# Where two norm averages and a row of products are written, and when four sums are made, in a kernel of two attention blocks

## The chip, the cores and the metric

The kernel runs on one core of a Trainium2 chip. A core has a TensorE (PE, the matmuls; PEld is its weight load), VectorE (DVE), ScalarE (ACT), GpSimdE (POOL) and SyncE (SP, which issues the DMAs). Matmuls write into PSUM, eight banks of 512 float32 for each of 128 partitions; VectorE and ScalarE read it from there. The metric is the device time of one execution in microseconds. One execution was profiled; in the text, times within it are counted from the start of its span.

## The reference, cut to what matters

The input x has 8 samples of 512 channels by 32 x 32 positions (1024 positions). Two layers follow each other:

```
# layer 0: 32 groups of 16 channels, 8 heads of 64 channels
h = group_norm(x, norm_w, norm_b)                  # mean and var over 16 channels x 1024
q, k, v = heads of (qkv_w @ h + qkv_b)
attn = softmax(q @ k.T / sqrt(64))                 # per head, 1024 x 1024
x = x + proj_w @ (attn @ v) + proj_b

# layer 1: one group of all 512 channels, one head
n = (x - mean(x)) * rsqrt(var(x) + eps) * gn_gamma + gn_beta
q, k, v = wq @ n + bq, wk @ n + bk, wv @ n + bv
attn = softmax(q.T @ k * 512**-0.5)                # 1024 x 1024
x = x + wo @ (v @ attn.T) + bo
```

All of it is float32.

## The kernel before, in words

The samples run one after the other, B = 8, each through `layer0` (from L651) and `attention1` (from L873). In layer 1 the weights are joined ahead of the loop: K's weight is multiplied into Q's (`wqk1`), and the output projection into V's (`wvo1`), by `product` (L581). Layer 1's norm is not applied to x: Q is made of raw x, and the norm comes in as a constant for each channel (`norm.c`) and a factor in the softmax. So the mean and the variance are needed only when the first finished parts of Q are scaled.

Large products are made by Strassen's scheme (`strassen`, L411), with seven multiplications of half size in place of eight. Each of the two operands is taken in quarters; of the weight the sums S1 to S4 are made (`finish`, L187), of the data T1 to T4 (`Combined.make`, L391: T1 = B12 - B11, T2 = B22 - T1, T3 = B22 - B12, T4 = B21 - T2). VectorE makes them all. One run of `strassen` is a generator of a group of output channels (or positions). It takes two PSUM tiles of two banks each, one with the tag "s" and one with the tag "o", and uses the first bank of each: `line` and `single`. Each tag has two tiles. The second bank of the "o" tile is left over and is remembered in `spare`. The order of one group is: A11·B11 into `line`, which ScalarE copies out (u1); A12·B21 into `single`, and VectorE adds u1 to it (`done(0, 0)`); S1·T1 into `single`; S2·T2 onto `line`, copied (u2); S3·T3 onto `line`, copied (u3), and `done(1, 1)`; A22·T4 onto `line`, `done(1, 0)`, then S4·B22 onto `single`, `done(0, 1)`.

`together` (L450) runs two such groups in turn, one piece of each: step 0 is the first piece of group 0, step 1 the first of group 1, step 2 the second of group 0 (S1·T1), step 3 that of group 1, steps 4 and 5 are S2·T2, 6 and 7 are S3·T3, 8 and 9 the rest. `at_steps` (L461) calls other work, the hooks, after the step whose number they have. As VectorE, ScalarE and TensorE take their instructions in the order in which the program issues them (`manual_schedule`, L1048), the step of a hook is its place in three queues at once. The DMA queue of SP is ordered by a planner.

Small matmuls that need a bank for a moment ask `room` (L279). It gives the spare bank if there is one. Both groups of `together` set `spare`, so from step 1 on it is the second group's. The users are:

- `group_average` (L283) and `sample_average` (L293), which average statistics over partitions with one matmul. `Norm.mean_of_all` (L322) and `Norm.deviation` (L332) call them, for the mean and the variance; in `deviation` POOL takes the power -0.5 afterwards.
- `through_q` (L1084), once, which multiplies the norm's and the bias's vectors into the joined Q weight (`Rows`, L551, 24 small matmuls), copies the rows out, stores them, and scales the weight's rows on ScalarE (L232).
- the row of biases `bias0` (L727) and the sums of `sum_both` (L815) for the next sample.

In `attention1` the Q stage (L903) makes Q in two groups, with T1 after step 0, the mean and T2 after step 1, the variance after step 3, and after step 4 `untaken` (four small constants), the two scaled products that were put off (`later`), and T3; T4 follows after step 6. V, the scores, the exponentials and the values come after it.

At the start of the program the Q and K weights of layer 0 are used for the first sample at L1101. Ahead of it stand `norm.normed` (x times scale plus shift), `wvo1.finish` (S1 to S4 of the joined V weight, and its store to DRAM), and `taken`, which copies the joined Q weight out of the four banks that the first Q and K use next. The weights live in a pool of three buffers (`wpool`), so `load_first("v0")` gets its buffer when an earlier weight is done with.

Of the kernel before, what the change touches and what calls it, by code (L numbers as in the profile page):

```python
# [65 lines left out]
def two_attention_blocks(  # L66
# [31 lines left out]
    def banks(tag, name):  # L98
        return psum.tile([P, 2, HALF], FP, tag=tag, name=name)
# [39 lines left out]
    nv1, wo1, nq1, nk1 = (raw(name) for name in ["nv1", "wo1", "nq1", "nk1"])  # L139
# [111 lines left out]
    waiting = []  # L251
# [24 lines left out]
        else:  # L276
            nc.scalar.copy(dst, src)

    def room(name):  # L279

        return banks("s", f"ps_{name}")[:, 0, :] if spare[0] is None else spare[0]

    def group_average(stat, name):  # L283

        ps = room(name)
        nc.tensor.matmul(
            ps[:, :NC], in_group.rearrange("p g s -> p (g s)"), stat, start=True, stop=True
        )
        mean = small.tile([P, NC], FP, tag="mean", name=f"mean_{name}")
        nc.vector.tensor_copy(mean, ps[:, :NC])  # L290
        return mean

    def sample_average(stat, name):  # L293

        ps = room(name)
        nc.tensor.matmul(ps[:, :NC], in_sample, stat, start=True, stop=True)
        mean = small.tile([P, 1], FP, tag="mean1", name=f"mean_{name}")
        nc.vector.tensor_reduce(mean, ps[:, :NC], AX.X, ALU.add)
        return mean
# [76 lines left out]
    def norm1(xs, b):  # L376
        return Norm(xs, sample_average, f"1_{b}")
# [28 lines left out]
            self.make(4)  # L406


    spare = [None]

    def strassen(multiply, done, name):  # L411

        us = {}

        def copied(n):
            us[n] = tile_u(f"u{n}_{name}")  # L420
            nc.scalar.copy(us[n], line)  # L421

        line = banks("s", f"ps_{name}_0")[:, 0, :]
        single = banks("o", f"ps_{name}_1")
        single, spare[0] = single[:, 0, :], single[:, 1, :]
        multiply(line, "A11", "B11", True)
        copied(1)
        multiply(single, "A12", "B21", True)
        done(0, 0, single, us[1])
        yield  # L430
        multiply(single, "S1", "T1", True)
        yield
        multiply(line, "S2", "T2", False)
        copied(2)
        yield
        multiply(line, "S3", "T3", False)
        copied(3)
        done(1, 1, single, us[3])
        yield
        multiply(line, "A22", "T4", False)  # L440
        done(1, 0, line, None)
        multiply(single, "S4", "B22", False)
        done(0, 1, single, us[2])
        yield
# [5 lines left out]
    def together(*groups):  # L450

        groups = list(groups)
        while groups:
            for g in list(groups):
                if next(g, g) is g:
                    groups.remove(g)
                else:
                    yield
        spare[0] = None

    def at_steps(steps, hooks):  # L461

# [188 lines left out]
    def layer0(bs, qs, ks, b, norm_next):  # L651
# [67 lines left out]
        ps = {}  # L719
# [17 lines left out]
        if norm_next is not None:  # L737
            hooks[4] = [lambda: norm_next.mean_of_all()]
            hooks[5] = [lambda: norm_next.variance_of_all()]
            combine = Combined(f"0_{b + 1}")  # L740
# [9 lines left out]
        norm = norm1(xs, b)  # L750
# [31 lines left out]
        for i in range(2, len(units) + 2):  # L782
# [4 lines left out]
            name = f"0_{b}_{pair}_{g}"  # L787
            if kt == NT - 1 and pair == end:
                if last:
                    ps_sum = banks("o", f"ps_sum_{name}")[:, 0, :]  # L790
# [13 lines left out]
        if b == 0:  # L804
            rows, = throughs
# [3 lines left out]
        if not last:  # L809

            name = f"0_{b}_{end}"
# [13 lines left out]
        later = []  # L825

        def project(w, c):
            def done(i, half, bank, u):
                chunk = c + 2 * i
                x = piece(xs, chunk, half)  # L830

                def add():
                    nc.vector.scalar_tensor_tensor(
                        x, bank if u is None else u, bias[:, chunk : chunk + 1], x, ALU.add, ALU.add
                    )
                    norm.of_half(chunk, half)


                first = last and i == half == 0
                if first and c == 0:  # L840
                    ps_sum = spare[0]
                    add_keys(end, [1], ps_sum)
                    combine1()
                    combine2(2, 0)
                    combine2(3, 0)
                if u is not None:
                    nc.vector.tensor_tensor(u, bank, u, ALU.add)
                if not first:
                    add()
                    return  # L850
                later.append(add)
                if c == 0:
                    invs[end] = one_over(ps_sum, f"0_{b}_{end}_1")
                    divide(end, 1, invs[end])
                else:

                    held(flat(accs[end, 1]), f"acc_0_{b}_{end}", flat(accs[end, 1]))
                    for n, k in [(2, 1), (3, 1), (4, 0), (4, 1)]:
                        combine2(n, k)
                    for more in later:  # L860
                        more()

            return strassen(by_channels(w, c, comb), done, f"p_0_{b}_{c}")
# [9 lines left out]
    def attention1(xs, norm, b, at_values):  # L873
# [5 lines left out]
        combine, later = Combined(f"1_{b}"), []  # L879
# [3 lines left out]
        def make_q(c):  # L883
# [18 lines left out]

        at_steps(together(make_q(0), make_q(1)), {  # L903
            0: [lambda: combine.make(1)],
            1: [norm.mean_of_all, lambda: combine.make(2)],
            3: [norm.deviation],
            4: [norm.untaken, lambda: later.pop(0)(), lambda: later.pop(0)(), lambda: combine.make(3)],
            6: [lambda: combine.make(4)],
        })
        bias = norm.bias()  # L910
        vs = blank(NT // 2, f"v_1_{b}")
# [12 lines left out]
        ps = [[[tile2(f"p_1_{b}_{j}{k}{i}") for i in range(2)] for k in range(2)] for j in range(2)]  # L924
# [65 lines left out]
        invs, later = [], []  # L990

        def values(c):
            def multiply(bank, a, b, fresh):
                for kt in range(NT // 2):
                    nc.tensor.matmul(  # L995
                        bank, v_parts[kt // 2][a][:, kt % 2, c * P : (c + 1) * P],
                        p_parts[kt // 2][b][:, kt % 2, :], start=fresh and kt == 0,
                        stop=kt == NT // 2 - 1, skip_group_check=True,
                    )

            def done(i, j, bank, u):
                first = i == j == 0
                if first and c == 0:
                    ps = spare[0]
                    for half in range(2):
                        nc.tensor.matmul(  # L1006
                            ps[half * HD : (half + 1) * HD, :], ones[:, :HD], acc[:, half, :],
                            start=True, stop=True,
                        )
                chunk = c + 2 * i  # L1010
                x = piece(xs, chunk, j)
                if u is None:
                    u = tile_u(f"o_1_{b}_{chunk}_{j}")
                else:
                    nc.vector.tensor_tensor(u, bank, u, ALU.add)
                    bank = u
                if first and c == 0:
                    held(ps, f"sum_1_{b}")
                    invs.append(one_over(ps, f"1_{b}"))
                    invs.append(spread(invs[0], HD, lambda i: [(i, r) for r in range(2)], f"1_{b}"))  # L1020

                def add():
                    nc.vector.scalar_tensor_tensor(
                        u, bank, norm.rstd, invs[1][:, j, :], ALU.mult, ALU.mult
                    )
                    nc.vector.scalar_tensor_tensor(
                        x, u, bias[:, chunk : chunk + 1], x, ALU.add, ALU.add
                    )

                if first:  # L1030
                    later.append(add)
                else:
                    add()

            return strassen(multiply, done, f"o_1_{b}_{c}")
# [9 lines left out]
    made, throughs = {}, []  # L1045


    with tc.manual_schedule(engines={PE, ACT, DVE}):  # L1048
        norm = norm0(xs_next, 0)
# [5 lines left out]
        wvo1 = Weight("wvo1")  # L1055
        product(wvo1, nv1, wo1, "o")()
        waiting.append(load_first("qk02"))
        wqk1 = Weight("wqk1")
        spare[0] = banks("o", "ps_norm")[:, 0, :]
        norm1_vectors = many(V_NB1, "norm1", V_NW1)  # L1060
        bias_v, bias_q = many(V_BV1, "bias_v", 0), many(V_BQ1, "bias_q", 0)

# [19 lines left out]
            throughs.append(Through(wvo1, bias_v, wo1, "v", banks("o", "ps_rows")[:, 0, :]))  # L1082

        def through_q():  # L1084
            throughs.append(Through(wqk1, bias_q, nk1, "q", room("rows")))

        taken = product(wqk1, nq1, nk1, "s", {
            (0, 1): [through_v], (1, 3): [norm.mean_of_all], (2, 1): [norm.variance_of_all]
        })
        spare[0] = None  # L1090
        norm.normed(xs_next)
        wvo1.finish()
        taken()
        waiting.append(load_first("v0"))
        ahead = [norm0(load_x(1, nc.sync), 1)]
        combine = Combined("0_0")
# [2 lines left out]
        qs, ks = [None] * NC, [None] * NC  # L1099
        w = next_weight()  # L1100
        at_steps(together(*pairs_qk(w, 0, combine.parts, qs, ks, 0)), {  # L1101
            1: [lambda: combine.make(3), through_q], 2: [lambda: combine.make(4)], 4: [wqk1.finish],
            8: [waiting[0].finish],
        })
        bs = combine.parts
        for rows in throughs:
# [1 line left out]
        for b in range(B):  # L1108
            if 0 < b < B - 1:
                ahead = [norm0(load_x(b + 1, nc.sync), b + 1)]  # L1110
            xs, norm, qs, ks = layer0(bs, qs, ks, b, ahead[0] if b + 1 < B else None)
# [24 lines left out]
        ps = banks("o", "ps_good")[:, 0, :]  # L1136
# [414 lines left out]
```

## Time and profile before

| what | value |
|---|---|
| median of 3 runs | 2943.11 us (2942.21 to 2943.16) |
| the profiled run, and its span | 2942.51 us, 2940.8 us |
| PE busy | 2906.7 us, 99% of the span |
| DVE busy | 1725.9 us, 59% |
| ACT busy | 1091.1 us, 37% |
| POOL busy | 14.2 us |
| from one V stage of layer 0 to the next sample's | 431.85 to 792.08 us, so 360.2 us |
| the Q stage of layer 1 in sample 1 | 643.65 to 670.40 us |

A line of the timeline has the start, the length, the engine, the line of the kernel, the operation, the tile that is written and those that are read, partitions and elements, and how many such instructions were merged. In square brackets stands how long the engine was idle before, and who ended that. In the chain of work that ended last, each piece has its start and its length. In a list of waits, the columns are the total in us, how often, and the longest. A float32 matmul shows as two records.

### The profile page before, as it was taken

Reading aid. Unit: us, or ns where it says so; the run is one execution under the profiler, and the core shown is the slowest. Engines: PE = TensorE matmul, PEld = TensorE weight load, DVE = VectorE, ACT = ScalarE, POOL = GpSimd, SP = SyncE. Lnnn points to the kernel's source line nnn. Section 1 sums busy time; section 2 is a strip of 40 time slices with the busy share of each in tenths; the row PEclk is TensorE's granted clock in tenths of the full one; section 3 lists DMA queues with packets and bytes.
Section 4 is the critical chain, followed back from the end, with each engine's and each line's share of the span. In section 5 each row is a group of like instructions: output and inputs, shape, how many; then the busy total and the mean of one; then the engine's idle time right before and its main releaser. Section 6 shows DMA issues by size and latency. Waiting matters only on the chain.

```text
span 2940.8 us, 34098 instructions
## 1 busy us (share of the span) xinstructions
PE 2906.7 (99%) x14050; PEld 1356.5 (46%) x14050; DVE 1725.9 (59%) x2147; ACT 1091.1 (37%) x1512; POOL 14.2 (0%) x28
## 2 busy tenths in 40 slices
PE   8999999999999999999999999999999999999998
PEld 4534544345543455334553355533545335453353
DVE  4676365853667536675367753577545764537835
ACT  2362324623246231552315523165222642226431
POOL 0000000000000000000000000000000000000000
PEclk9999999999999999999999999999999999999999
DMA  6401122011220112202031020310212111111001
GB/s 232 180 18 62 50 80 93 23 58 50 93 80 22 58 51 93 87 16 80 27 118 62 15 82 27 117 62 22 75 54 89 64 42 67 48 68 55 8 1 37
DMA packets 70724, 188.74 MB, mean 64 GB/s; under 512 B 18464, under 2 KB 18976, under 8 KB 64160
## 3 DMA queue, kind: packets, MB, share of 16 engines
q1 hardware_dynamic: 70416, 186.46, 18.9%
q8 instruction: 112, 1.84, 0.3%
q14 instruction: 52, 0.43, 0.1%
q10 hardware_dynamic: 144, 0.02, 0.0%
HBM read 137.43 MB, written 28.57 MB: 56 GB/s over the span
## 4 chain that ended last, share of the span: by engine, by line
PE 97%; DVE 2%; ACT 0%; issue 0%; SPq 0%; DMA 0%; POOL 0%; DVEq 0%; ACTq 0%; POOLq 0%
PE s L677 15%; PE ps_o L696 15%; PE ps_v L489 13%; PE ps_o L995 13%; PE ps_s L938 13%; PE ps_q L474 13%; PE ps_k L474 7%; PE ps_p L474 6%; PE ps_sum L710 1%; PE ps_wvo L589 1%; DVE u_q L887 0%; DVE inv L619 0%; DVE t L397 0%; PE ps_o L1006 0%; DVE acc L608 0%; PE ps_wqk L589 0%
## 5 line engine op out<-in xcount | busy, mean ns | idle before, releaser
L606 ACT ACTIVATE p<-s 128x1024 f32<-128x1024 f32 x512 | 523.8, 1025 | 316.2 <-PE s L677 313.5
L677 PE MATMUL s<-q,k 64*64 64x512 f32 x4096 | 532.2, 591 | 0.0
L696 PE MATMUL ps_o<-p,v 64*64 64x512 f32 x4096 | 528.7, 589 | 0.0
L608 DVE TENSOR_TENSOR acc<-acc,p 128x1024 f32<-128x1024 f32 x384 | 468.6, 1220 | 86.2 <-ACT p L606 69.9
L677 PEld LDWEIGHTS s<-q,k 64*64 64x64 f32 x4096 | 152.6, 133 | 292.9 <-issue 258.3
L696 PEld LDWEIGHTS ps_o<-p,v 64*64 64x64 f32 x4096 | 156.6, 133 | 282.8 <-issue 280.3
L946 DVE TENSOR_TENSOR p<-ps_s,u_s 128x512 f32<-128x512 f32 x96 | 66.4, 692 | 246.8 <-ACT u_s L421 140.9
L523 DVE TENSOR_TENSOR v<-ps_v,u_v 128x512 f32<-128x512 f32 x96 | 66.2, 690 | 197.6 <-PE ps_v L489 126.3
L421 ACT COPY u_v<-ps_v 128x512 f32<-128x512 f32 x96 | 56.3, 586 | 305.8 <-PE ps_v L489 305.8
L938 PE MATMUL ps_s<-s_q,t 128*128 128x512 f32 x384 | 167.4, 592 | 0.0
L995 PE MATMUL ps_o<-t_p,s_v 128*128 128x512 f32 x384 | 166.1, 592 | 0.0
L421 ACT COPY u_q<-ps_q 128x512 f32<-128x512 f32 x96 | 56.0, 583 | 272.8 <-PE ps_q L474 272.8
L608 DVE TENSOR_TENSOR acc<-p,p 128x1024 f32<-128x1024 f32 x64 | 78.4, 1225 | 98.9 <-ACT p L606 98.9
L474 PE MATMUL ps_q<-t,w_wqk 128*128 128x512 f32 x256 | 116.8, 600 | 7.3 <-DVE t L397 7.3
L948 ACT ACTIVATE p<-p,factor 128x512 f32<-128x512 f32 x96 | 69.3, 722 | 133.2 <-DVE p L946 133.2
L938 PEld LDWEIGHTS ps_s<-s_q,t 128*128 128x128 f32 x384 | 73.0, 190 | 91.8 <-issue 91.8
L995 PEld LDWEIGHTS ps_o<-t_p,s_v 128*128 128x128 f32 x384 | 73.0, 190 | 91.8 <-issue 87.3
L995 PE MATMUL ps_o<-p,v 128*128 128x512 f32 x256 | 113.3, 595 | 0.0
L474 PE MATMUL ps_p<-t_p,w_p 128*128 128x512 f32 x256 | 112.6, 593 | 0.7 <-DVE inv L619 0.7
L489 PE MATMUL ps_v<-w_wvo,t 128*128 128x256 f32 x512 | 113.1, 379 | 0.0
L938 PE MATMUL ps_s<-q,x 128*128 128x512 f32 x256 | 112.5, 592 | 0.0
L315 DVE BATCH_NORM_STATS2 part<-x 128x6 f32<-128x512 f32 x128 | 85.4, 687 | 35.0 <-DMA x<-in_x 32.7
(226 smaller groups left out, 3564.6 us busy)
## 6 DMA issues: line engine op xcount, KB each, us to landing
x<-in_x SPq DMA_DIRECT2D x92, 512.0 KB, 7.3
w_qk<-stored_qk SPq DMA_DIRECT2D x14, 1792.0 KB, 7.4
out<-x SPq DMA_DIRECT2D x32, 512.0 KB, 2.8
inv<-inv SPq DMA_DIRECT2D x248, 64.0 KB, 2.0
w_wqk<-stored_wqk SPq DMA_DIRECT2D x8, 1792.0 KB, 7.6
w_wvo<-stored_wvo SPq DMA_DIRECT2D x8, 1792.0 KB, 7.2
w_v<-stored_v SPq DMA_DIRECT2D x7, 1792.0 KB, 7.1
w_p<-stored_p SPq DMA_DIRECT2D x7, 1792.0 KB, 7.2
```

The costliest lines, as they stand in the source:

```text
L315: nc.vector.bn_stats(self.part[:, cc, half, :], piece(self.xs, cc, half))
L421: nc.scalar.copy(us[n], line)
L474: nc.tensor.matmul(bank, w[a][:, k, c * P : (c + 1) * P], bs[b][:, k, :], start=fresh and k == 0, stop=k == 1, skip_group_check=True,)
L489: nc.tensor.matmul(bank[:, u * 2 * P : (u + 1) * 2 * P], bs[b][:, k, n * P : (n + 1) * P], w[a][:, k, :], start=fresh and u == k == 0, sto ...
L606: nc.scalar.activation(p, s, AF.Exp, scale=factor)
L608: nc.vector.tensor_tensor(acc, first, p, ALU.add)
L677: nc.tensor.matmul(s[cols, j, :], flat(ks[pair])[rows, k0 : k0 + HD], qs[pair][rows, g, :], start=True, stop=True,)
L696: nc.tensor.matmul(o[cols, half, :], vs[kt][rows, c0 : c0 + HD], p[rows, j, :], start=kt == 0, stop=kt == NT - 1,)
L938: nc.tensor.matmul(bank, bs[b][:, k, t * P : (t + 1) * P], q_parts[a][:, k, :], start=fresh and k == 0, stop=k == 1, skip_group_check=True,)
L946: nc.vector.tensor_tensor(p, bank, u, ALU.add)
L948: nc.scalar.activation(p, bank, AF.Exp, scale=norm.factor)
L995: nc.tensor.matmul(bank, v_parts[kt // 2][a][:, kt % 2, c * P : (c + 1) * P], p_parts[kt // 2][b][:, kt % 2, :], start=fresh and kt == 0, ...
```

## The change

`spare`, one place, becomes `spares`, a list with the left-over bank of each group that runs. `room` takes a number: the norm averages and `through_q` ask for the first group's bank, the other callers still get the latest one. In the Q stage of layer 1 the mean goes from step 1 to step 2, T3 from step 4 to 2, the variance from step 3 to 4, T4 from step 6 to 4, and the constants with the two scaled products from step 4 to 5. At the start, `wvo1.finish` goes from ahead of `taken` to step 3 of the first Q and K, `through_q` from step 1 to step 2, there ahead of T4, and `wqk1.finish` from step 4 to step 5.

```diff
@@ -276,13 +276,13 @@
         else:
             nc.scalar.copy(dst, src)
 
-    def room(name):
-
-        return banks("s", f"ps_{name}")[:, 0, :] if spare[0] is None else spare[0]
+    def room(name, n=-1):
+
+        return spares[n] if spares else banks("s", f"ps_{name}")[:, 0, :]
 
     def group_average(stat, name):
 
-        ps = room(name)
+        ps = room(name, 0)
         nc.tensor.matmul(
             ps[:, :NC], in_group.rearrange("p g s -> p (g s)"), stat, start=True, stop=True
         )
@@ -292,7 +292,7 @@
 
     def sample_average(stat, name):
 
-        ps = room(name)
+        ps = room(name, 0)
         nc.tensor.matmul(ps[:, :NC], in_sample, stat, start=True, stop=True)
         mean = small.tile([P, 1], FP, tag="mean1", name=f"mean_{name}")
         nc.vector.tensor_reduce(mean, ps[:, :NC], AX.X, ALU.add)
@@ -406,7 +406,7 @@
             self.make(4)
 
 
-    spare = [None]
+    spares = []
 
     def strassen(multiply, done, name):
 
@@ -422,7 +422,8 @@
 
         line = banks("s", f"ps_{name}_0")[:, 0, :]
         single = banks("o", f"ps_{name}_1")
-        single, spare[0] = single[:, 0, :], single[:, 1, :]
+        spares.append(single[:, 1, :])
+        single = single[:, 0, :]
         multiply(line, "A11", "B11", True)
         copied(1)
         multiply(single, "A12", "B21", True)
@@ -450,13 +451,14 @@
     def together(*groups):
 
         groups = list(groups)
+        spares.clear()
         while groups:
             for g in list(groups):
                 if next(g, g) is g:
                     groups.remove(g)
                 else:
                     yield
-        spare[0] = None
+        spares.clear()
 
     def at_steps(steps, hooks):
 
@@ -838,7 +840,7 @@
 
                 first = last and i == half == 0
                 if first and c == 0:
-                    ps_sum = spare[0]
+                    ps_sum = spares[0]
                     add_keys(end, [1], ps_sum)
                     combine1()
                     combine2(2, 0)
@@ -902,10 +904,10 @@
 
         at_steps(together(make_q(0), make_q(1)), {
             0: [lambda: combine.make(1)],
-            1: [norm.mean_of_all, lambda: combine.make(2)],
-            3: [norm.deviation],
-            4: [norm.untaken, lambda: later.pop(0)(), lambda: later.pop(0)(), lambda: combine.make(3)],
-            6: [lambda: combine.make(4)],
+            1: [lambda: combine.make(2)],
+            2: [norm.mean_of_all, lambda: combine.make(3)],
+            4: [norm.deviation, lambda: combine.make(4)],
+            5: [norm.untaken, lambda: later.pop(0)(), lambda: later.pop(0)()],
         })
         bias = norm.bias()
         vs = blank(NT // 2, f"v_1_{b}")
@@ -1001,7 +1003,7 @@
             def done(i, j, bank, u):
                 first = i == j == 0
                 if first and c == 0:
-                    ps = spare[0]
+                    ps = spares[0]
                     for half in range(2):
                         nc.tensor.matmul(
                             ps[half * HD : (half + 1) * HD, :], ones[:, :HD], acc[:, half, :],
@@ -1056,7 +1058,7 @@
         product(wvo1, nv1, wo1, "o")()
         waiting.append(load_first("qk02"))
         wqk1 = Weight("wqk1")
-        spare[0] = banks("o", "ps_norm")[:, 0, :]
+        spares.append(banks("o", "ps_norm")[:, 0, :])
         norm1_vectors = many(V_NB1, "norm1", V_NW1)
         bias_v, bias_q = many(V_BV1, "bias_v", 0), many(V_BQ1, "bias_q", 0)
 
@@ -1082,14 +1084,12 @@
             throughs.append(Through(wvo1, bias_v, wo1, "v", banks("o", "ps_rows")[:, 0, :]))
 
         def through_q():
-            throughs.append(Through(wqk1, bias_q, nk1, "q", room("rows")))
+            throughs.append(Through(wqk1, bias_q, nk1, "q", room("rows", 0)))
 
         taken = product(wqk1, nq1, nk1, "s", {
             (0, 1): [through_v], (1, 3): [norm.mean_of_all], (2, 1): [norm.variance_of_all]
         })
-        spare[0] = None
         norm.normed(xs_next)
-        wvo1.finish()
         taken()
         waiting.append(load_first("v0"))
         ahead = [norm0(load_x(1, nc.sync), 1)]
@@ -1099,8 +1099,8 @@
         qs, ks = [None] * NC, [None] * NC
         w = next_weight()
         at_steps(together(*pairs_qk(w, 0, combine.parts, qs, ks, 0)), {
-            1: [lambda: combine.make(3), through_q], 2: [lambda: combine.make(4)], 4: [wqk1.finish],
-            8: [waiting[0].finish],
+            1: [lambda: combine.make(3)], 2: [through_q, lambda: combine.make(4)],
+            3: [wvo1.finish], 5: [wqk1.finish], 8: [waiting[0].finish],
         })
         bs = combine.parts
         for rows in throughs:
```

## The prediction

> **What bounds the kernel now.** I read the page first: busy shares, then the chain that ended last.
>
> ```profile
> span 2940.8 us, 34098 instructions
> PE 2906.7 (99%) x14050; PEld 1356.5 (46%) x14050; DVE 1725.9 (59%) x2147; ACT 1091.1 (37%) x1512; POOL 14.2 (0%) x28
> PE 97%; DVE 2%; ACT 0%; issue 0%; SPq 0%; DMA 0%; POOL 0%; DVEq 0%; ACTq 0%; POOLq 0%
> ```
>
> TensorE sets the end. The change removes no large matmul, so only two things can pay: time in which TensorE stands still, and time at a lower clock. Next I asked for all waits, and kept those of PE:
>
> ```profile
> PE ps_q L474 <- DVE t L397: 7.3, 8, 0.9
> PE ps_q L296 <- DVE u_q L887: 6.8, 8, 0.9
> ```
>
> Both occur eight times, once a sample, in the Q stage of the second layer, which the change edits. The PE timeline of sample 1's stage:
>
> ```profile
> 643.65 7.03 PE L474 MATMUL ps_q<-x,w_wqk 128*128 128x512 f32 x16
> 651.54 0.39 PE L296 MATMUL ps_q<-stat,in_sample 128*128 128x4 f32 x2 [0.85 <-DVE u_q L887]
> 651.78 3.68 PE L474 MATMUL ps_q<-t,w_wqk 128*128 128x512 f32 x8
> 655.30 0.28 PE L296 MATMUL ps_q<-spread,in_sample 128*128 128x4 f32 x2
> 655.44 7.11 PE L474 MATMUL ps_q<-t,w_wqk 128*128 128x512 f32 x16
> 663.46 1.95 PE L474 MATMUL ps_q<-t,w_wqk 128*128 128x512 f32 x4 [0.91 <-DVE t L397]
> ```
>
> The last rows of this stage end where V begins, at 670.40. A 512-column record takes 0.429 us from start to start (663.46 to 665.25 holds four, with a slow first). The stage takes 670.40 - 643.65 = 26.75 us for 56 such records, which is 24.03; 2.72 us are something else. The chain in the same stretch says what:
>
> ```profile
> 650.79 0.70 DVE u_q L887
> ...
> 660.87 0.60 ACT u_q L421
> 661.47 0.02 issue
> 661.49 0.69 DVE u_q L887
> 662.18 1.14 DVE t L397
> ```
>
> The mean's matmul waits for the second group's sum u_q to be read out of the bank beside it; T4 stands in VectorE's queue behind a u_q that needs ScalarE's copy.
>
> The third place is the start, once. The chain from 20 to 70 us:
>
> ```profile
> 35.75 0.61 DVE w_wvo L188
> ...
> 38.28 0.61 DVE rest_wqk L599
> 38.89 0.04 issue
> 38.94 5.40 PE ps_q L474 x8
> ...
> 47.87 0.76 DVE k L506
> 48.64 0.14 issue
> 48.77 1.96 PE ps_k L551 x24
> ```
>
> Four sums of wvo (35.75 to 38.28) stand ahead of the copy that frees the first Q's bank, and the vectors' products wait for k's sum. Its first eight matmuls take 5.40 us instead of 3.43; a stage table over that stretch gives the granted clock, 0.67, after PE's busy time:
>
> ```profile
> 39.00:44.10 5.10, 5.10 (x8) 2.13 (x9) 5.00 (x10) 0.59 (x1) 0.00 (x0) 0.67 1.02 360
> ```
>
> **The Trainium skill.** "PSUM — Partial Sum Buffer", section "PSUM bank collisions raise a hardware error", says to guard PSUM by bank (and quadrant), not address. The trace is stricter: the mean's matmul waits 0.85 us for a read of the other bank of its two-bank tile, so the wait follows the tile. "TensorE: Matmul & The Clock Gate", section "What's actually happening", says an idle window of about 3.4 us halves the array's clock for the next, and that windows run freely. The trace agrees roughly: 2.04 us of idleness before 38.94 was followed by the half clock, while 2.44 us before 115.75 was not (granted clock 1.00 from 92.1 to 121.4). The same page (section "Architectural detail: the array is 16× 32×32, not 1× 128×128") calls VectorE and ScalarE strict FIFO; T4's place agrees. "DMA: Bandwidth & Descriptors", section "Issuing engines are not separate DMA queues", says that all transfers share 16 engines: a stored_qk at 47.48 and rows_q at 51.40 agree, rows_q taking 10.0 us to land against 2.0 for rows_v.
>
> **The change, Q stage, eight times.** Take PE's end of the first 16 records, 643.65 + 16 x 0.429 = 650.52. New order: group 0's S1·T1 to 652.24 (T1 ready at 649.25), then the mean's pair. It writes group 0's tile, last read at 648.12, and its statistics are ready: no wait. A pair costs 0.14 plus a slow start of about 0.09 (group norm's pairs at 104.12 and 106.06 do just that), so 0.23. Group 1's S1·T1 to 654.2; group 0's S2·T2 to 655.9 (T2 now directly follows u_q, ready near 652.7); the variance's pair (spread ready near 653.5); group 1's S2·T2 to 657.8. T3 runs on DVE near 653.5 to 654.7, needed at 657.8. T4 follows the variance's small operations, near 656.6 to 657.8, instead of 663.3; needed at 661.3.
>
> What is queued behind: on DVE the four constants (about 0.7 us) now wait for T4, so they end near 658.4 instead of 657.37; POOL's power (0.55 us) moves a step and overlaps T4. On ACT the two scaled products (1.52) now follow group 1's copy, to 660.0, and group 0's third copy (0.59) ends near 660.6. Its line is written again at 661.3: 0.7 us of slack, so I cost it at nothing, hidden by group 1's S3·T3. The held u buffers: five exist; the sixth request comes after the first scaled product. Result 24.03 + 2 x 0.23 = 24.48; gain 26.75 - 24.48 = 2.27 a sample, bounds 1.1 (ACT takes T4's place) to 2.72 (the pairs cost nothing). Times eight: 18.2 us. V, scores and the rest follow PE, so all shifts.
>
> **Group norm of the next sample** merely moves to q's spare bank. Its pairs waited for nothing before and q's sum is read long before: nothing, hidden in PE's stream.
>
> **The start.** ACT's copies of the K product begin at 36.67; DVE's copy of the same bank follows ACT's (as wvo's at 21.13 did), so it ends near 37.95 rather than 38.88: Q starts at 38.0, gain 0.9. PE then idles 1.1 us instead of 2.04, and I expect the full clock: gain 4 x 0.43 = 1.7. q and k end near 44.9. The vectors' products go after q's S1·T1 into q's tile, read near 44.5: the k wait (1.00 plus a slow start, 1.17) goes. Sum 3.8. Row copy and eight scalings on ACT (0.59 and 8 x 0.40) end near 52.7, and q's second copy follows at 53.3, 0.3 before PE needs its line: nothing. wqk's sums (4 x 0.6) run to 55.2, before q's third copy: nothing.
>
> Moved with wvo's sums is its store, and what waits on that:
>
> ```profile
> 38.34 0.33 SPq L238 DMA_DIRECT2D stored_wvo<-w_wvo  x1
> ...
> 45.11 0.34 SPq L216 DMA_DIRECT2D w_v<-in_s_v  x1
> ```
>
> w_v's load waits for the store's landing (6.8 us), as it takes its buffer. New sums run near 48.0 to 50.5 (behind T3 and T4 on DVE), the store lands near 57.4, w_v needs 5.5 more: 62.9 alone. But wqk's store (1792 KB, issue near 55.3) shares the DMA engines: near 64.5. V could start at 63.9 to 64.1. So 0 to 1.5 us come back; I take 0.5. SP itself no longer stands 6.6 us before the first store, so the x loads leave earlier and use idle DMA; rows_q and the small column loads have 40 us to spare. v's own sums wait with w_v on DVE, behind them k's last sum; V's second group asks for k's bank only about 5 us later: hidden. Start: 3.8 - 0.5 = 3.3, bounds -1 and 4.
>
> **Sum** against the profiled span: 2940.8 - 18.2 - 3.3 = 2919.3. The timed runs' median, 2943.1, is 2.3 over that span (the profiled run itself took 2942.5), so 2921.5.
>
> **Rivals.** (a) *w_v late.* For it: DMA moved 312 to 422 GB/s between 48 and 56 us, and SP issues in order, so w_v may stand behind a wait for rows_q. Then V starts at 67 to 68 and the start gives 0 to 1: 2943.1 - 18.2 - 0.5, about 2924.5; worse still if the x loads follow the late store, about 2928. (b) *ACT becomes T4's successor*: the third copy waits behind the scaled products by 1.5 us or more, and only the mean's wait goes: 8 x 1.1 + 3.3, so 2931. Against it: 0.7 us of slack in every sample. (c) *Slower*: the constants come late behind POOL's power and T4, the scaled products block ACT, and group 0's A22·T4 waits. It decides when the constants end over 0.7 + 2.27 + 0.41 = 3.4 us after 658.4, past 661.8; for slower by 0.2% (5.9 us) past 662.5; at 663 about 2953. Against it: from the variance's matmul to the constants took 655.30 to 657.37, 2.1 us, and T4 adds only 1.2. (d) *It doesn't do what it says*: the two waits are merely renamed (the bank choice isn't what held the mean, T4 waits for another sum): 2940 with the start's gain.
>
> **How the numbers follow.** Main 0.64, (a) 0.20, (b) 0.08, (c) 0.05, (d) 0.03. 0.2% is 5.9 us, about what a measurement of this kernel can tell from no change. Faster holds main, (a), (b): 0.92; same 0.03; slower 0.05. The main case's own range is 2917 (all 2.72 us of the Q stage and 4 at the start gone: 25.8) to 2925; with (a) 2917 to 2929.
>
> **What would show it.** Right: 24.4 to 24.6 us from the first Q matmul to V in each sample, no PE wait on u_q L887 or t L397, T4 finished about 3 us before its matmul; Q of the first sample at 38.0, at full clock; products named ps_q directly after the first T1 matmuls. Wrong: a PE or PEld wait on an ACT copy near A22·T4 (b, c); a PE wait on w_v near 64 us (a). A period per sample other than 360.2 - 2.3 = 357.9 us would mean that a step outside the Q stage moved, which I exclude.

## The result, and the profile after

The changed kernel takes 2923.53 us (median of 4 runs, 2923.14 to 2924.43) against 2943.14 us before (2942.21 to 2943.37). The ratio is 0.9934, with a 95% interval of 0.9917 to 0.9952: 19.6 us, or 0.7%, faster. The forecast was 2921.5 us in a range of 2917 to 2929.

The page of the changed kernel still shows TensorE as the bound:

```profile
span 2921.4 us, 34110 instructions
PE 2901.8 (99%) x14050; PEld 1357.2 (46%) x14050; DVE 1725.5 (59%) x2147; ACT 1090.7 (37%) x1512; POOL 21.0 (1%) x28
PE 97%; DVE 1%; DMA 1%; ACT 0%; SPq 0%; issue 0%; POOL 0%; DVEq 0%; ACTq 0%; POOLq 0%
```

Two things differ besides the span: the DMA share of the chain has gone from 0% to 1%, and POOL's busy time has grown by half. Both return below. All waits of PE that the trace of the changed kernel shows:

```profile
PE ps_wvo L591 <- DMA wo<-in_w_o: 4.6, 1, 4.6
PE ps_good L1137 <- DVE good L1135: 2.8, 1, 2.8
PE ps_k L553 <- DVE many_bias L538: 2.4, 1, 2.4
PE ps_v L491 <- DMA w_v<-in_s_v: 1.2, 1, 1.2
PE ps_q L476 <- DVE rest_wqk L601: 1.1, 1, 1.1
PE ps_p L476 <- DVE inv L621: 0.8, 1, 0.8
```

The same list of the kernel before has, besides the two waits that occur eight times:

```profile
PE ps_q L474 <- DVE rest_wqk L599: 2.0, 1, 2.0
PE ps_k L551 <- DVE k L506: 1.0, 1, 1.0
```

The two that occurred eight times are gone, and so is the one on k's sum. One is new, on the load of v's weight; the one on rest_wqk fell from 2.0 to 1.1. The PE timeline of the Q stage of sample 1 (two lines higher in the numbering than before):

```profile
648.58 0.28 PE L296 MATMUL ps_q<-stat,in_sample 128*128 128x4 f32 x2
648.72 3.68 PE L476 MATMUL ps_q<-t,w_wqk 128*128 128x512 f32 x8
652.23 0.28 PE L296 MATMUL ps_q<-spread,in_sample 128*128 128x4 f32 x2
652.37 7.11 PE L476 MATMUL ps_q<-t,w_wqk 128*128 128x512 f32 x16
659.32 1.88 PE L476 MATMUL ps_q<-x,w_wqk 128*128 128x512 f32 x4
```

No line has an idle time in brackets. The stage runs from 639.99 to 664.47, so 24.48 us instead of 26.75, and the time from one sample's V to the next is 786.15 - 428.19 = 357.96 us instead of 360.2. Eight times 2.27 is 18.2 of the 19.4 us that the span lost. The rest, 1.2 us, is about what the start gives: V of the first sample begins at 66.46 instead of 67.93 us. The PE timeline of the kernel before, and then the chain of the changed kernel:

```profile
67.93 4.26 PE L489 MATMUL ps_v<-w_v,x 128*128 128x256 f32 x19
```


```profile
38.88 3.70 PE ps_q L476 x8
42.58 3.43 PE ps_k L476 x8
46.01 1.72 PE ps_q L476 x4
47.73 1.95 PE ps_q L553 x24
...
53.34 6.17 DMA stored_wvo<-w_wvo
59.51 0.02 issue
59.53 6.80 DMA w_v<-in_s_v
66.32 0.14 issue
66.46 5.63 PE ps_v L491 x25
```

The first eight Q matmuls take 3.70 us, not 5.40, and the products follow q's S1·T1 without a gap. Then the chain leaves PE: the store of the joined V weight and the load of v's weight after it decide when V starts.

### The profile page after: what moved, and what is told of

Its sections match the earlier page's. It is cut to its first block, busy times and chain, and to the rows that moved or that the text cites. A ratio compares the mean times of both kernels' runs of the same rounds, so it can differ in the third digit from the quotient of the medians.

```text
span 2921.4 us, 34110 instructions
## 1 busy us (share of the span) xinstructions
PE 2901.8 (99%) x14050; PEld 1357.2 (46%) x14050; DVE 1725.5 (59%) x2147; ACT 1090.7 (37%) x1512; POOL 21.0 (1%) x28
## 4 chain that ended last, share of the span: by engine, by line
PE 97%; DVE 1%; DMA 1%; ACT 0%; SPq 0%; issue 0%; POOL 0%; DVEq 0%; ACTq 0%; POOLq 0%
PE s L679 15%; PE ps_o L698 15%; PE ps_v L491 13%; PE ps_o L997 13%; PE ps_s L940 13%; PE ps_q L476 13%; PE ps_p L476 6%; PE ps_k L476 6%; PE ps_sum L712 1%; PE ps_wvo L591 1%; DVE inv L621 0%; PE ps_o L1008 0%; DVE acc L610 0%; PE ps_wqk L591 0%; PE ps_k L712 0%; DMA w_v<-in_s_v 0%
```

## The experiments

**The Q stage alone** keeps the start as it was, so it separates the two places.

```diff
         norm.normed(xs_next)
+        wvo1.finish()
         taken()
 ...
-            1: [lambda: combine.make(3)], 2: [through_q, lambda: combine.make(4)],
-            3: [wvo1.finish], 5: [wqk1.finish], 8: [waiting[0].finish],
+            1: [lambda: combine.make(3), through_q], 2: [lambda: combine.make(4)], 4: [wqk1.finish],
+            8: [waiting[0].finish],
```

(`through_q` asks for the latest bank again.)

> The changed kernel's Q stage of layer 1 and its first-group bank for the norm averages; the start (joined V weight's sums, vectors' products) as before. Theory: the Q stage is worth 2.26 us a sample and nothing else in the loop moved, so 2943.1 - 8 x 2.26 = 2925.0 us, stage 24.5 us, and the start shows 2.0 us of PE idleness before the first Q and half the clock for its first matmuls, as before. Rival: part of the 18 us comes from the start (sums out of the way of later work), then 2928 us or more.

Measured: 2924.59 us, ratio to before 0.9938 (0.9921 to 0.9954), and a stage of 666.20 - 641.72 = 24.48 us. The theory holds: the Q stage carries nearly all of the gain. About 1 us by the medians is left for the start, which these runs do not tell from nothing (2923.84 to 2924.71 us here, 2923.14 to 2924.43 with the changed start). The half clock came back, as a stage table of this run shows (granted clock after PE, PEld, DVE, ACT and POOL busy):

```profile
38.90:44.50 5.60, 5.24 (x9) 2.20 (x9) 5.50 (x11) 0.58 (x1) 0.00 (x0) 0.70 0.93 328
```

**The start alone** has the old hooks in the Q stage and the latest bank for the averages.

```diff
-        ps = room(name, 0)     # both averages
+        ps = room(name)
 ...
-            1: [lambda: combine.make(2)],
-            2: [norm.mean_of_all, lambda: combine.make(3)],
-            4: [norm.deviation, lambda: combine.make(4)],
-            5: [norm.untaken, lambda: later.pop(0)(), lambda: later.pop(0)()],
+            1: [norm.mean_of_all, lambda: combine.make(2)],
+            3: [norm.deviation],
+            4: [norm.untaken, lambda: later.pop(0)(), lambda: later.pop(0)(), lambda: combine.make(3)],
+            6: [lambda: combine.make(4)],
```

> The changed start alone; Q stage of layer 1 and the averages' bank as before. Theory: V of the first sample starts 1.5 to 2.3 us earlier than before, held by the load of v's weight (PE wait of about 1.2 us), so 2941.5 us, within 0.1% of before. Without the half clock at the first Q. Rival: the start gives the full 3.8 us of its parts, because the wait for v's weight is not caused by the later store but was a disturbance of one execution: 2939.3 us.

Measured: 2941.56 us, ratio 0.9996 (0.9987 to 1.0004): not to be told from before by time, so it is the trace that decides. V of the first sample starts at 66.25 instead of 67.93 us, and the same wait for v's weight stands before it:

```profile
66.25 4.12 PE L491 MATMUL ps_v<-w_v,x 128*128 128x256 f32 x18 [1.18 <-DMA w_v<-in_s_v]
```

So that wait belongs to the changed start and is not the accident of one execution.

**The bank alone**: the changed kernel's first-group bank for the averages, with the old hooks in the Q stage (as above) and the old start (as in the first experiment).

> Only the bank: averages go beside the first group's sums, with the old order of the Q stage (mean after step 1) and the old start. Theory (a wait follows the two-bank tile, both ways): the mean's matmul no longer waits for u_q, but group 0's S1.T1, next on PE, writes the same tile and has to wait until VectorE has read the mean, which stands behind u_q in its queue. Stage 26.7 us as before, about 2943 us; PE's wait is renamed (on the reduce of the mean). Rival (the bank alone removes the mean's wait): 8 x 1.0 us less, 2935 us, stage 25.7 us.

Measured: 2941.64 us, ratio 0.9996 (0.9988 to 1.0005); the stage takes 670.85 - 644.26 = 26.59 us. The wait was renamed. PE timeline of this kernel, then the chain of the same moment:

```profile
651.12 0.28 PE L296 MATMUL ps_q<-stat,in_sample 128*128 128x4 f32 x2
652.21 3.70 PE L476 MATMUL ps_q<-t,w_wqk 128*128 128x512 f32 x8 [0.80 <-DVE mean_m L298]
```

```profile
651.39 0.69 DVE u_q L889
652.09 0.08 DVE mean_m L298
652.17 0.04 issue
652.21 3.70 PE ps_q L476 x8
```

The mean's matmul starts at once, but the following S1·T1 writes the first bank of the same tile and must wait until the mean has been read, behind u_q. The choice of bank by itself is worth nothing measurable.

**The order alone**: the new hooks with the averages in the second group's bank (`room(name)` in both), and the old start.

> Only the order of the Q stage (T3, T4 earlier, mean after step 2, variance after step 4), with the averages in the second group's bank and the old start. Theory (wait follows the tile, both ways): the mean's matmul waits for nothing, but group 1's S1.T1, next on PE, writes the tile in which the mean stands and waits for its reduce, 0.5 to 0.7 us a sample; stage 25.0 to 25.2 us, about 2929 to 2930 us. Rival (order does it all, the bank is irrelevant): as with the bank, stage 24.5 us, 2925 us.

Measured: 2927.76 us, ratio 0.9950 (0.9933 to 0.9967); stage 666.41 - 641.51 = 24.90 us. The list of PE's waits has one in this stage that the changed kernel lacks:

```profile
PE ps_q L476 <- DVE mean_m L298: 2.0, 8, 0.3
```

The theory's mechanism is there, at less than its expected price: T2 and the reduce end only 0.25 us after PE is ready, and the stage is 24.90 - 24.48 = 0.42 us longer, not 0.5 to 0.7. That is 3.4 us in all, against 3.2 us between the medians of this kernel and of the first experiment. So the order gives about 1.85 us a sample and the bank, once the order is right, 0.42.

**The norm half of the Q stage alone**, with the first group's bank and the old start; T3 and T4 stay at their old steps.

```diff
-            2: [norm.mean_of_all, lambda: combine.make(3)],
-            4: [norm.deviation, lambda: combine.make(4)],
+            2: [norm.mean_of_all],
+            4: [norm.deviation, lambda: combine.make(3)],
             5: [norm.untaken, lambda: later.pop(0)(), lambda: later.pop(0)()],
+            6: [lambda: combine.make(4)],
```

> The Q stage's norm half alone, with the first group's bank: mean after step 2, variance after 4, constants after 5; T3 after step 4 and T4 after step 6, as before; old start. Theory: the two waits are separate; the mean's goes (about 1.1 us a sample), T4's stays. Stage 25.6 us, 2943 - 8 x 1.1 = 2934 us. Rival: T4's wait grows, because the scaled products now stand ahead of the third copy that T4's predecessor on VectorE needs: stage 26 us or more, 2937 us or more.

Measured: 2937.22 us, ratio 0.9980 (0.9974 to 0.9987); stage 668.35 - 642.35 = 26.00 us. The rival holds. The mean's wait went, but T4's grew from 7.3 to 9.6 us over the eight samples:

```profile
PE ps_q L476 <- DVE t L397: 9.6, 8, 1.2
```

The chain of this kernel runs through the constants and the scaled products:

```profile
655.40 1.41 POOL rstd L336
...
657.41 1.52 ACT q L893 x2
658.93 0.48 ACT u_q L421
659.41 0.02 issue
659.44 0.69 DVE u_q L889
660.13 1.14 DVE t L397
```

The two halves of the change are thus not independent. Moving the norm later puts the scaled products ahead of the third copy, and as long as T4 queues behind the u_q that needs this copy, part of the gain (about 0.3 us a sample) is handed back. T4 made early takes that link out. The other half, T3 and T4 early with the norm at its old steps, was not run.

**The joined V weight's sums two steps earlier**, in the changed kernel:

```diff
-            1: [lambda: combine.make(3)], 2: [through_q, lambda: combine.make(4)],
-            3: [wvo1.finish], 5: [wqk1.finish], 8: [waiting[0].finish],
+            1: [wvo1.finish, lambda: combine.make(3)], 2: [through_q, lambda: combine.make(4)],
+            5: [wqk1.finish], 8: [waiting[0].finish],
```

> The changed kernel with the joined V weight's sums two steps earlier, ahead of T3 (step 1 instead of 3). Theory: the first V waits 1.2 us because v's weight takes the buffer of the joined V weight, whose store left SP at 53.3 us, behind the wait for the rows' landing and two column loads. Sums earlier end near 49.4, the store goes ahead of the rows, v's weight lands near 62 to 63 instead of 66.3, no PE wait before V, V starts 1.2 us earlier against the first Q: 2922.3 us. Rival: v's weight is bound by the DMA engines, which it shares with the joined Q weight's store; it lands at most 0.5 us earlier and PE still waits: 2923.3 us.

Measured: 2920.92 us, ratio 0.9926 (0.9911 to 0.9941). PE's wait for w_v is gone, and from the first Q to V it is 63.65 - 37.41 = 26.24 us instead of 66.46 - 38.88 = 27.58. That gains 1.34 us; by the medians this kernel is 2.6 us ahead of the changed one. The rest is about what its profiled execution shows ahead of the first Q, which starts 1.47 us earlier without the edit's doing (see under "Why the prediction was right"). SP's queue of this kernel:

```profile
48.00 0.33 SPq L238 DMA_DIRECT2D stored_wvo<-w_wvo  x1
48.85 0.32 SPq L562 DMA_DIRECT2D rows_q<-row_q  x1
54.24 0.33 SPq L216 DMA_DIRECT2D w_v<-in_s_v  x1
54.74 0.32 SPq L238 DMA_DIRECT2D stored_wqk<-w_wqk  x1
```

In the changed kernel the same queue stood otherwise:

```profile
50.32 0.33 SPq L562 DMA_DIRECT2D rows_q<-row_q  x1
52.33 0.92 SPq L570 DMA_DIRECT2D c_q<-rows_q  x2
53.34 0.45 SPq L238 DMA_DIRECT2D stored_wvo<-w_wvo  x1
56.21 0.33 SPq L238 DMA_DIRECT2D stored_wqk<-w_wqk  x1
59.53 0.33 SPq L216 DMA_DIRECT2D w_v<-in_s_v  x1
```

The sums ended at 51.67 there, but their store stood 1.67 us behind the landing of the rows and two column loads; and w_v followed wqk's store and needed 6.8 us from issue to landing, against 5.5 when it went ahead of it. By these figures the earlier departure is enough: counted from the first Q, v's load left after 16.83 us instead of 20.65, 3.8 us earlier, and the wait to be removed was 1.2.

**The bias vectors made early**, in the changed kernel. This is a wait that the change left alone.

```diff
         bias_v, bias_q = many(V_BV1, "bias_v", 0), many(V_BQ1, "bias_q", 0)
+        bias0_vectors = many(V_BV0, "bias0")
 ...
-                rows = Rows([(many(V_BV0, "bias0"), p0.moving)], 1, "bias0", room("bias0"))
+                rows = Rows([(bias0_vectors, p0.moving)], 1, "bias0", room("bias0"))
```

> The changed kernel, with the tile of bias vectors for the row of biases made at the start with the others, not in VectorE's queue behind the projection weight's sums. A one-time PE wait of 2.4 us, left alone by the change, should go: 2921.1 us. Rival: k's bank or the scores' bank then holds PE instead, and the wait is renamed: 2923.5 us.

Measured: 2919.94 us, ratio 0.9922 (0.9907 to 0.9937). The 2.4 us wait is gone and no other took its place. By the medians this kernel is 3.6 us ahead of the changed one; the 1.2 beyond the wait was not followed up.

**Both of these edits**:

> Both edits of the two kernels before (sums at step 1, bias vectors early), which lie in different places: 1.2 + 2.4 us, so 2919.9 us. If v's weight is bound by the DMA engines, 2921.

Measured: 2917.39 us (2917.20 to 2918.09), ratio 0.9915 (0.9901 to 0.9928). It is the fastest kernel of this study: 25 us below before. Its lead over the changed kernel, 6.1 us by the medians, comes from two separate comparisons with before, whose intervals overlap; its span, 2915.5 against 2921.4, says the same. Of the 5.9 us between the spans, the two waits removed explain 1.34 + 2.44. Another 1.5 is that the first Q itself begins earlier (37.36 against 38.88), which neither edit touches (see under "Why the prediction was right"); the remaining 0.6 was not followed up.

**T4 one step earlier still**, in the changed kernel, to see what lengthened POOL's work:

```diff
-            4: [norm.deviation, lambda: combine.make(4)],
+            3: [lambda: combine.make(4)],
+            4: [norm.deviation],
```

> The changed kernel with T4 after step 3, ahead of the variance's small operations, instead of after step 4 behind them. Theory: POOL's power took 1.40 us instead of 0.55 because VectorE ran T4, an addition of two SBUF tiles, beside it; with T4 out of the way it takes 0.55 again and the constants end 0.7 to 0.9 us earlier against the variance's matmul. PE does not wait there, so the stage stays 24.5 us. Rival: the power is longer because it runs at another place (its operands' arrival), then it stays 1.40.

Measured, in one run: 2922.36 us, stage 664.31 - 639.83 = 24.48 us. POOL's power, in the changed kernel and in this one:

```profile
653.04 1.40 POOL L336 TENSOR_TENSOR rstd<-rstd,minus_half 128x1 f32<-128x1 f32 x1 [185.04 <-DVE rstd L335]
```

```profile
652.88 0.55 POOL L336 TENSOR_TENSOR rstd<-rstd,minus_half 128x1 f32<-128x1 f32 x1 [185.04 <-DVE rstd L335]
```

The theory holds: T4, a subtraction of two SBUF tiles that ran from 652.82 to 654.04, was what lengthened it. In the experiment on the norm half T3, also made of two SBUF tiles, ran there, and the power took 1.40 us too.

## Why the prediction was right, and where it was off

*The Q stage.* Forecast 24.48 us and 357.9 us a sample; measured 24.48 and 357.96. Both waits vanished as worked out, and the mechanism behind the first held: the bank alone and the order alone show a wait that follows the two-bank tile in both directions. The prediction named only one direction, the small matmul that waits for a read of its neighbour. The other, the next large matmul that waits for the read of the small one, is what makes the order necessary.

*The slack on ScalarE.* Put at 0.7 us with a power of 0.55 us. The power took 1.40, the constants ended 2.9 us after the variance's matmul (652.23 to 655.15) instead of 2.5, and group 0's third copy ended at 657.05. Its line was written again at 652.37 + 0.09 + 12 x 0.429 = 657.6, so about 0.55 us was left. Rivals (b) and (c) did not occur, yet the experiment on the norm half shows that (b)'s mechanism is real where T4 stays late.

*The start.* PE's idleness before Q fell from 2.04 to 1.12 us as forecast, the first matmuls ran at full clock, and the wait on k's sum went. From the first Q to V, 28.99 us became 27.58, of which 1.34 is the wait for v's weight with its slow restart; without it, 26.24. The mis-sized term is that wait, put at 0.5 of a bound of 0 to 1.5. Its chain was right (the buffer, the store, the shared engines), but the main sum left out SP's order, which only rival (a) names, with a wait for the rows: the store left at 53.34 instead of about 50.5. By the prediction's own sign, a PE wait on w_v near 64 us, rival (a) is what came at the start, in a milder form: PE stood still from 65.28, and V began at 66.46, not at 67 to 68. So the forecast of the start was right in its range and not in its main case.

*The 2.0 us by which the forecast was too low.* In the profiled execution two terms make up most of it. The wait for v's weight accounts for 0.8. The other, about 0.9, lies before anything that the change touches: the same 32 matmul records of the first product took 16.77 us in the timeline, not 15.85, and Q's whole stretch starts later by nearly that. The weight loads show where: they start 0.85 us apart at first and 0.43 us apart afterwards, and the turn comes later in the changed kernel. The timeline of PEld before, then of the changed kernel:

```profile
8.17 0.32 PEld L589 LDWEIGHTS ps_wvo<-wo,nv 128*128 128x128 f32 x1 [0.52 <-issue]
8.72 0.19 PEld L589 LDWEIGHTS ps_wvo<-wo,nv 128*128 128x128 f32 x1 [0.24 <-issue]
```

```profile
9.82 0.34 PEld L591 LDWEIGHTS ps_wvo<-wo,nv 128*128 128x128 f32 x1 [0.52 <-issue]
10.45 0.19 PEld L591 LDWEIGHTS ps_wvo<-wo,nv 128*128 128x128 f32 x1 [0.29 <-DMA nq<-in_n_q]
```

The first Q matmuls of the kernel before have the same 0.85 us at the half clock. That it is the clock here too is read from the spacing alone, as the stage tables show 1.00 for this stretch. The moment of the turn does not follow the edits: the product lasts 15.47 us with both edits and 16.70 with the start alone, both with a changed start, and 16.77 with the bank alone, which has the old one. What sets it was not tested.

*The half clock.* "I expect the full clock" held, but the gain is less sure than a sum can say. In the five profiled kernels that have the 2.0 us gap before Q, the half clock followed it in three (before, the Q stage alone, the bank alone). In the other two (the order alone, the norm half) it came 75 us later, after the 2.4 us wait on the bias vectors, as a stage table of the order alone shows:

```profile
112.00:117.00 5.00, 2.98 (x24) 0.98 (x24) 4.33 (x6) 0.58 (x1) 0.00 (x0) 0.67 0.65 275
```

In the six kernels whose first gap is 1.1 us none shows it there, and the four of them that still have the wait on the bias vectors don't show it after that one either. So a gap of 2 us costs up to 1.7 us more in some executions, which fits the free-running windows of the Trainium skill's page "TensorE: Matmul & The Clock Gate", section "What's actually happening"; that the phase decides was inferred and not tested. The page speaks of an idle window of about 3.4 us; here gaps of 2.04 to 2.44 us were enough.

## What to carry to other kernels

A bank that is free is not the same as a bank that can be written without a wait: here the wait went by the tile (whether the banks themselves would have allowed the access earlier was not tested), so a small matmul has to be placed in the queue where the tile's last read lies behind it and the tile's next write lies some matmuls ahead. When a step moves later, look at what now queues behind it, and move the link that depends on it (here T4) in the same edit. A store whose buffer the next weight takes is part of that weight's path, and so is everything that SP issues between the two.

## What was not expected of the hardware

POOL's power of one column took 1.40 us instead of 0.55 while VectorE subtracted two SBUF tiles (1.22 us), and 0.55 again with that subtraction moved away. The Trainium skill's page "SBUF — State Buffer", section "Who interferes with whom", says just this: a VectorE instruction with two SBUF inputs contends with a GpSimd instruction that reads SBUF. These runs agree, with 0.85 us as the price of one such meeting; as PE did not wait for it, it cost no time here.
